# All router logits of a Mamba, MLP and mixture-of-experts layer on VectorE instead of TensorE

## The chip, the core and the metric

The kernel runs on one core of one Trainium2 chip. The metric is the device time of one execution in microseconds (us). All data is fp32. The engines are called as the profile calls them: PE (TensorE, the matrix multiplies), PEld (its weight loads), DVE (VectorE), ACT (ScalarE), POOL (GpSimd) and SP (SyncE, which here only issues DMAs). Each engine runs its own instructions in order and waits for the others through semaphores.

## What is computed

The input is one sequence of 2048 tokens with 512 channels. Two layers follow each other, each behind a layer norm and with a residual:

```python
x = L0_attn_hidden_states
x = x + _L0_attn_ref(_layernorm(x, axis=-1), ...)   # Mamba2 mixer, then a gated MLP
x = x + _L0_ffn_ref(_layernorm(x, axis=-1), Wr, Wg, Wu, Wd)
```

The first layer is a Mamba2 mixer (projection to 2576 columns, causal convolution of four taps, chunked state-space scan with 16 heads and chunks of 128 tokens, gated norm, output projection) and an MLP with 2048 hidden channels. The second is a mixture of eight experts with 352 hidden channels, of which every token takes two:

```python
router_logits = jnp.einsum('bsh,he->bse', x, Wr)       # x: normed tokens, Wr: 512 x 8
probs = jax.nn.softmax(router_logits.astype(jnp.float32), axis=-1)
topk_w, topk_idx = jax.lax.top_k(probs, K)             # K = 2
topk_w = topk_w / jnp.sum(topk_w, axis=-1, keepdims=True)
...
h = jax.nn.silu(g) * u                                  # g, u: x through Wg, Wu of each expert
y = jnp.einsum('besi,eih->besh', h, Wd)
out = jnp.einsum('bse,besh->bsh', combine.astype(x.dtype), y)
```

The change is about the first line only: the 2048 x 8 router logits.

## The kernel before, in words

**Stages.** Tokens are handled in tiles of 128 (on the partitions). The mixer runs in 8 blocks of 256 tokens (`mamba`, two `chunk`s each), the MLP in 4 blocks of 512 tokens (`feed_forward(fb)`, `fb` = 0 to 3, four tiles each). The MLP of block `fb` is interleaved with the mixer of the following tokens; the last MLP block stands after the mixer, next to the loads of the expert weights (`load_expert`). Then come the expert tiles (`tiles`, 36 slots of 128 gathered tokens), which add their output to `out` by indirect DMA.

**Order.** Both stages are Python generators that yield after a piece of work. `advance` moves the MLP on by one step per step of the mixer. PE keeps the program's order from the third mixer block on (`tc.manual_schedule`); the other engines and SP's DMA queue are ordered by a scheduler that estimates when each instruction can run. `tc.high_priority(AT_ONCE)` and `tc.issue_after(x)` bend that order by hand.

**The MLP block.** It has 16 parts `c` of 128 hidden channels, four steps each. A part is seven products of a 2 x 2 block scheme (`product`, L735), into two PSUM banks `x1` and `x2`. VectorE adds or multiplies the results: L768 (`p3`), L794 (`up`), L762 (`p2`) and L799. POOL multiplies gate by up (L800). From the third part on, two parts at a time are multiplied by the down weights (`mlp_down`, L719), and VectorE adds that to the token rows (L720). The weights come in through SP: `mg` (early, L534) and `ms` (late, L547) share three buffers, `md` (L552) has four. The mixer's weights `wi` (L99) have three. In the first block `mg` and `ms` are built from `w_gu`.

**The router, the end of each MLP block.** `route(fb, rows)` runs as the `tail` beside the next MLP block, one step of it per four steps of that block. It takes the layer norm of each tile (`normed`, L603), writes the normed tile `xn` to DRAM (`xnd`, and `xnd1` for blocks 0 to 2) and the residual to `out`. For blocks 0 to 2 it transposes `xn` on PE (four transposes, L201), copies the result to `xT` on ACT (L203), and multiplies it by the router's weights `wr_sb` (L612, four matmuls with 8 columns, recorded as 8), whose result DVE copies out (L613). For block 3 it computes logits on DVE: for each expert `e`, row `wr_rows[e]` is spread over all partitions (`cols`, L630), and `dot` (L616) multiplies a tile by it and sums. Then `top` picks two experts, matmuls with `tri` and `ones` (`pr`, L682 and L683) count the tokens ahead of each token, and POOL scatters token lists to DRAM (L697).

**From lists to experts.** `table(NS1, "1")` continues the tail of block 2: it makes the tile table of the first 16 expert slots, loads the lists (L1003) and ends with `idx` (L1014), by which POOL gathers the tokens of the first slots (L1054). This has to be ready when block 3's MLP ends.

**Buffers.** `mid` is a pool of three 2 KB (per partition) buffers, for `xn`, `xT`, small tables and the experts' `eh`. `row` has five. `params` holds convolution weights, biases, norms and the `D` vector in 116 columns and is loaded at the start.

Of the kernel before, what the change touches and what calls it, by code (L numbers as in the profile page):

```python
# [9 lines left out]
F32 = mybir.dt.float32  # L10
I32 = mybir.dt.int32
AF = mybir.ActivationFunctionType
ALU = mybir.AluOpType
# [33 lines left out]
EPS = 1e-5  # L47


C_CW, C_CB, C_NW, C_D, C_L1, C_L2, C_DTB, C_AL = 0, 48, 60, 68, 76, 80, 84, 100  # L50
NPAR = 116


@with_exitstack
def mamba_mlp_moe(ctx, tc, x, w_in, w_out, w_gu, w_down, par, wr, wr_rows, wg, wu, wd, out):

# [26 lines left out]
        nc.sync.dma_start(out=res[t], in_=x[t * P : (t + 1) * P, :])  # L83

    params = pw.tile([P, NPAR], F32, name="params")
    w_dt = pw.tile([P, NK, NH], F32, name="w_dt")
    w_o = pw.tile([P, 8, D], F32, name="w_o")
    wr_sb = const.tile([P, NK, NE], F32, name="wr_sb")

    for t in range(2 * NCH):  # L90
        load_x(t)
# [8 lines left out]
        return w  # L100

    ahead = [load_w_in(pair) for pair in range(2)]
    nc.sync.dma_start(out=wr_sb, in_=wr.rearrange("(k p) e -> p k e", p=P))


    ident = const.tile([P, P], F32, name="ident")
# [288 lines left out]
    def chunk(b, j, dt, ncum, dtdec, cd, cum, ec, xb, cs, zs):  # L395
# [9 lines left out]
        for gp in range(2):  # L405

            if t:
                with tc.issue_after(summed), tc.high_priority(AT_ONCE):
                    nc.gpsimd.tensor_tensor(ec[:, gp], ec[:, gp], cs[gp][:, :, tok], ALU.mult)
# [39 lines left out]
            if gp == 0 and t < NT - 1:  # L449
                pst = ps_tr.tile([P, 2, 4, HD], F32, name=f"pst{t}", tag="tr")  # L450
                for g in range(4):
                    nc.tensor.matmul(pst[halves[g % 2], g // 2], xbt[:, 1, g, :], xd[:, g], start=True, stop=True)


            yd = wa.tile([P, 4, P], F32, name=f"yd{t}_{gp}", tag="y")
            for i in range(4):
                at = C_D + 4 * gp + i
                nc.vector.scalar_tensor_tensor(
                    yd[:, i, :], xb[:, gp, tok], params[:, at : at + 1], py[:, i, :], ALU.mult, ALU.add
                )  # L460
            nc.vector.tensor_tensor(y[:, 4 * gp : 4 * gp + 4, :], yd, y[:, 4 * gp : 4 * gp + 4, :], ALU.mult)

# [50 lines left out]
        transposed(h, h2T[fb][:, half, :, off : off + P], params[:, C_L2 : C_L2 + NK])  # L513

# [55 lines left out]
    nc.gpsimd.memset(zero, 0.0)  # L570
# [15 lines left out]

    def route(fb, rows):

        mv2, rs2 = small("mv2", NJ, 2), small("rs2", NJ)
        for j in range(NJ):  # L590
            stats(small_p, rows[j], mv2[:, j, :])
# [3 lines left out]
        if fb == NFB - 1:  # L595

            kept = wk.tile([P, NJ, D], F32, name="kept", tag="h2T", bufs=1)

        def normed(j):
            t = fb * NJ + j  # L600
            nc.scalar.dma_start(out=out[t * P : (t + 1) * P, :], in_=rows[j])
            xn = kept[:, j] if fb == NFB - 1 else mid([D], f"xn{t}")
            nc.vector.tensor_scalar(xn, rows[j], mv2[:, j, 0:1], rs2[:, j : j + 1], ALU.subtract, ALU.mult)  # L603
            nc.scalar.dma_start(out=xnd[t * P : (t + 1) * P, :], in_=xn)
            if fb < NFB - 1:
                nc.scalar.dma_start(out=xnd1[t * P : (t + 1) * P, :], in_=xn)
            return xn

        def logits(j, xT):
            pl = bank("d", [NE], f"pl{fb}_{j}")  # L610
            for k in range(NK):
                nc.tensor.matmul(pl, xT[:, k, :], wr_sb[:, k, :], start=(k == 0), stop=(k == NK - 1))  # L612
            nc.vector.tensor_copy(lg[:, j, :], pl)  # L613

        def dot(product, xn, col, j, e):
            nc.vector.scalar_tensor_tensor(  # L616
                product, xn, 1.0, col, ALU.mult, ALU.mult, accum_out=lg[:, j, e : e + 1]
            )

        if fb == NFB - 1:  # L620

# [5 lines left out]
            for e in range(NE):  # L627
# [1 line left out]
                    cols = pmlp.tile([P, 2, D], F32, name=f"cols{e}", tag="mg", bufs=3)  # L629
                    nc.sync.dma_start(out=cols, in_=bc(wr_rows[e : e + 2], 0, P))  # L630
                for j in range(NJ):

                    with tc.issue_after(turning):
                        dot(pmlp.tile([P, D], F32, name="dot", tag="md", bufs=4), kept[:, j], cols[:, e % 2], j, e)
# [79 lines left out]

    def mlp_down(fb, rows, j, pair):

        pd = bank("d", [D], f"pd{fb}_{j}")
        for m, (a, d) in enumerate(pair):
            nc.tensor.matmul(pd, a[:, j * P : (j + 1) * P], d, start=(m == 0), stop=(m == 1))  # L719
        nc.vector.tensor_tensor(rows[j], rows[j], pd, ALU.add)  # L720

    def feed_forward(fb):

        nonlocal mlp_w, newest
        if fb == 0:
            w = load_early(0, 0)
            mlp_w = w, load_late(0, 0, w)
# [15 lines left out]
        for c in range(NFC):  # L743
# [13 lines left out]
            x2 = bank("u", [FH], f"py{fb}_{c}")  # L757

            def p2():
                product(x2, late[:, 2], b21)  # L760
                with tc.high_priority(AT_ONCE):
                    nc.vector.tensor_tensor(a[:, 0], a[:, 0], x2, ALU.add)  # L762
                nc.scalar.activation(a[:, 0], a[:, 0], AF.Silu)

            def p3():
                product(x2, late[:, 1], b22, False)
                with tc.high_priority(AT_ONCE):
                    nc.vector.tensor_tensor(a[:, 1], a[:, 1], x2, ALU.add)  # L768
                nc.scalar.activation(a[:, 1], a[:, 1], AF.Silu)

            def p5():
# [19 lines left out]
            yield  # L791
            product(x1, late[:, 0], t3, False)
            with tc.high_priority(AT_ONCE):
                nc.vector.tensor_tensor(up, up, x1, ALU.add)  # L794
            order[2]()
            yield
            product(x1, late[:, 3], t4, False)
            with tc.high_priority(AT_ONCE):
                nc.vector.tensor_tensor(a[:, 0], a[:, 0], x1, ALU.mult)  # L799
# [37 lines left out]
    def weigh(n):  # L837

        for m in unweighted[:n]:
            tc.keep_in_program_order(  # L840
                nc.gpsimd.tensor_scalar_mul(w_o[:, m, :], w_o[:, m, :], params[:, C_NW + m : C_NW + m + 1])
            )
        del unweighted[:n]

# [60 lines left out]
    def advance():  # L905
# [158 lines left out]
    def hidden(s, xT):  # L1064
# [6 lines left out]
        for k in range(NK):  # L1071
# [153 lines left out]
```

## Time and profile before

| what | value |
|---|---|
| time, median of 3 runs | 1542.44 us (1539.53 to 1543.87) |
| profiled execution, time | 1538.42 us |
| its span | 1536.6 us |
| PE busy | 1494.7 us, 97% of the span |
| DVE busy | 766.3 us, 50% |
| ACT busy | 741.8 us, 48% |
| POOL busy | 425.3 us, 28% |
| DMA | 219.63 MB, mean 143 GB/s |
| mean granted clock of TensorE | 0.993 |

The profile is of one execution. The span is the time from the first to the last instruction; 1.8 us of the time lie around it. A line of a group names the kernel's line, the engine, the operation and the tiles (`out<-in`); after `x` stands how often. In the row of 40 slices each digit is the busy share of 38.4 us in tenths. A matmul in fp32 is recorded as two passes, except the transposes. Numbers in brackets behind an instruction are idle time of its engine ahead of it, with what ended it. `PEclk` or the column behind the engines is the granted clock as a share of full speed.

### The profile page before, as it was taken

To read this page: it belongs to the slowest core of one execution; us is meant where nothing else is said; L and a number is where in the kernel's file an instruction comes from. 1 tells how busy PE (TensorE), PEld (TensorE's weight loads), DVE (VectorE), ACT (ScalarE), POOL (GpSimd) and SP (SyncE) were. 2 spreads that over 40 slices of the span, in tenths; PEclk is the share of its full clock that TensorE was granted. 3 is DMA by queue.
4 is the path that set the end of the run, shared out by engine and by line. 5 is a ranking of instruction groups with operands and counts; after the bars stand their busy time and mean duration, and the time that the engine had idled before them with its cause. 6 is when DMAs were issued, how large, how long until landed. Compare 5 with 4: busy or idle time off the path is not lost. (4 is left out here: it accounts for less than half of the span.)

```text
span 1536.6 us, 18795 instructions
## 1 busy us (share of the span) xinstructions
PE 1494.7 (97%) x6105; PEld 1016.5 (66%) x6105; DVE 766.3 (50%) x1999; ACT 741.8 (48%) x1328; POOL 425.3 (28%) x537
## 2 busy tenths in 40 slices
PE   8899999999999999999999999999999999999996
PEld 6656567677667676767676677666776666656553
DVE  7676875645545564556545544435343345322221
ACT  5887976735663598457755754222221121211110
POOL 3442324423342212141213120411121123433321
PEclk9999999999999999999999999999999999999999
DMA  9443445545454553454435442426879643443332
GB/s 297 127 157 117 145 134 182 196 144 168 164 170 148 179 167 128 131 126 137 145 96 193 150 138 81 103 77 200 296 228 242 209 119 64 61 73 67 64 62 35
DMA packets 128817, 219.63 MB, mean 143 GB/s; under 512 B 12624, under 2 KB 72912, under 8 KB 128720
## 3 DMA queue, kind: packets, MB, share of 16 engines
q1 hardware_dynamic: 105952, 168.44, 36.0%
q0 software_dynamic: 9088, 18.91, 7.3%
q10 hardware_dynamic: 13680, 31.07, 5.4%
q8 instruction: 51, 0.84, 0.2%
q14 instruction: 46, 0.38, 0.1%
HBM read 177.58 MB, written 40.80 MB: 142 GB/s over the span
## 5 line engine op out<-in xcount | busy, mean ns | idle before, releaser
L719 PE MATMUL pd<-md,a 128*128 128x512 f32 x512 | 239.8, 595 | 0.8 <-DVE r L720 0.7
L340 PE MATMUL pm<-hT,wi 128*128 128x256 f32 x768 | 187.0, 389 | 3.8 <-DMA wi<-in_w_in 3.8
L720 DVE TENSOR_TENSOR r<-r,pd 128x512 f32<-128x512 f32 x128 | 87.5, 684 | 151.7 <-PE pd L719 150.9
L340 PEld LDWEIGHTS pm<-hT,wi 128*128 128x128 f32 x768 | 143.0, 193 | 29.7 <-issue 11.1
L719 PEld LDWEIGHTS pd<-md,a 128*128 128x128 f32 x512 | 97.4, 191 | 77.4 <-issue 66.6
L361 DVE SCALAR_TENSOR_TENSOR ca<-pre,params,ca 128x256 f32<-128x256 f32 x288 | 139.5, 541 | 0.3
L735 PE MATMUL py<-h2T,ms 128*128 128x256 f32 x512 | 131.7, 379 | 2.4 <-DMA ms<-late 1.7
L800 POOL TENSOR_TENSOR a<-a,up 128x256 f32<-128x256 f32 x64 | 47.1, 736 | 267.3 <-DVE up L794 234.4
L340 PE MATMUL pz<-hT,wi 128*128 128x256 f32 x512 | 117.0, 381 | 0.0
L490 PE MATMUL po<-w_o,zs 128*128 128x512 f32 x256 | 114.5, 600 | 0.0
L1074 PE MATMUL epg<-ew,xgT 128*128 x288 | 109.0, 460 | 0.2 <-issue 0.2
L1074 PE MATMUL epu<-ew,xgT 128*128 x288 | 108.7, 459 | 0.0
L735 PEld LDWEIGHTS py<-h2T,ms 128*128 128x128 f32 x512 | 95.5, 190 | 18.1 <-issue 2.4
L420 ACT ACT_TABLE_LOAD x75 | 96.2, 1283 | 21.0 <-DVE ncum L285 14.1
L340 PEld LDWEIGHTS pz<-hT,wi 128*128 128x128 f32 x512 | 94.8, 190 | 13.8 <-issue 0.8
L1096 PE MATMUL epd<-ew,ehT 128*128 (+1 forms) x216 | 99.0, 594 | 1.0 <-DVE ehT L1089 1.0
L420 ACT ACTIVATE cum<-cum,ncum 128x128 f32<-128x128 f32 x256 | 85.7, 392 | 6.0 <-POOL cum L314 4.4
L490 PEld LDWEIGHTS po<-w_o,zs 128*128 128x128 f32 x256 | 48.9, 192 | 57.4 <-issue 56.1
L780 ACT COPY a<-px 128x256 f32<-128x256 f32 x64 | 23.6, 369 | 129.3 <-PE px L735 112.4
L1054 POOL DMA_INDIRECT xg<-xnd,idx x36 | 35.6, 988 | 161.3 <-PE pt L201 157.0
L422 DVE SCALAR_TENSOR_TENSOR cum<-cum,dt,psc 128x128 f32<-128x128 f32 x256 | 72.9, 339 | 5.3 <-PE psc L414 3.0
L1074 PEld LDWEIGHTS epu<-ew,xgT 128*128 128x128 f32 x288 | 54.7, 190 | 30.5
(243 smaller groups left out, 2503.3 us busy)
## 6 DMA issues: line engine op xcount, KB each, us to landing
wi<-in_w_in SPq DMA_DIRECT2D x80, 512.0 KB
ms<-late SPq DMA_DIRECT2D x48, 512.0 KB
mg<-early SPq DMA_DIRECT2D x48, 384.0 KB
md<-in_w_down SPq DMA_DIRECT2D x64, 256.0 KB
cum<-rowsd SPq DMA_DIRECT2D x32, 512.0 KB
late<-ms ACTq DMA_DIRECT2D x16, 512.0 KB
ec<-rowsd SPq DMA_DIRECT2D x60, 128.0 KB
mg<-in_w_gu SPq DMA_DIRECT2D x48, 128.0 KB
```

The costliest lines, as they stand in the source:

```text
L340: nc.tensor.matmul(pm[:, m, :], w[:, k, m * P : (m + 1) * P], hT[:, k, :], start=(k == 0), stop=(k == NK - 1))
L361: nc.vector.scalar_tensor_tensor(ca, pre[:, m, k : k + TB], cw[:, k : k + 1], ca, ALU.mult, ALU.add)
L420: nc.scalar.activation(lt[:, half, i], lt[:, half, i], AF.Exp, bias=ncum[:, j, h : h + 1])
L422: nc.vector.scalar_tensor_tensor(lt[:, half, i], lt[:, half, i], dt[:, j, h : h + 1], psc[:, half, i], ALU.mult, ALU.mult)
L490: nc.tensor.matmul(po, y[:, m, :], w_o[:, m, :], start=(m == 0), stop=(m == 7))
L719: nc.tensor.matmul(pd, a[:, j * P : (j + 1) * P], d, start=(m == 0), stop=(m == 1))
L720: nc.vector.tensor_tensor(rows[j], rows[j], pd, ALU.add)
L735: nc.tensor.matmul(ps, w[:, k], m[:, k], start=(first and k == 0), stop=(k == KH - 1), skip_group_check=True)
L800: nc.gpsimd.tensor_tensor(a[:, 1], a[:, 1], up, ALU.mult)
L1054: nc.gpsimd.indirect_dma_start(out=xg, out_offset=None, in_=src, in_offset=bass.IndirectOffsetOnAxis(ap=idx[:, n : n + 1], axis=0))
L1074: nc.tensor.matmul(ps, xT[:, k, :], w[:, lo : lo + EI], start=(k == 0), stop=(k == NK - 1))
L1096: nc.tensor.matmul(pd, hT[:n, m, :], w[:n, NG + m * D : NG + (m + 1) * D], start=(m == 0), stop=(m == len(ET) - 1))
```

## The change

- The router's logits of blocks 0, 1 and 2 are computed by VectorE, as those of block 3 are. The transposes, the copies to `xT`, the router's matmuls and the copies of `pl` go, and with them the tile `wr_sb`.
- Blocks 0 and 1 go a tile at a time: the fourth tile first, whose `xn` is still in SBUF, then the other three, each read back from DRAM (`again`). For each of the 32 pairs of tile and expert the router's row is loaded again (`column`), and the product is written over it.
- Block 2 takes two tiles at a time (2 and 3, then 0 and 1 read back), with 8 columns for each pair of tiles and the product in a buffer of its own.
- A column's buffer is one of two (`col`); `mid` shrinks from three buffers to one, and the experts' `eh` moves to `col`.
- While there are dots to do (`quick`), the tail takes a step at every step of the MLP block and not at every fourth.
- Each dot is ordered after `turning`, now the latest VectorE instruction of the MLP block.
- `params` is split: `norm_w`, `D` and `ln2_w` go to `params2`, which is loaded in the place of `wr_sb`.

```diff
-    wr_sb = const.tile([P, NK, NE], F32, name="wr_sb")
+    params2 = pw.tile([P, NPAR2], F32, name="params2")
...
-    nc.sync.dma_start(out=wr_sb, in_=wr.rearrange("(k p) e -> p k e", p=P))
+    nc.sync.dma_start(out=params2, in_=par2)
...
     def mid(shape, name):
-        return wk.tile([P, *shape], F32, name=name, tag="mid", bufs=3)
+        return wk.tile([P, *shape], F32, name=name, tag="mid", bufs=1)
+
+    def col(name, shape=(D,)):
+        return wk.tile([P, *shape], F32, name=name, tag="col", bufs=2)
...
+        def place_of(j):
+            if fb == NFB - 1:
+                return kept[:, j]
+            if j == NJ - 1:
+                return row(f"xn{fb}_{j}") if fb == NFB - 2 else mid([D], f"xn{fb}_{j}")
+            if j == NJ - 2 and fb == NFB - 2:
+                return mid([D], f"xn{fb}_{j}")
+            return col(f"xn{fb}_{j}")
...
-        def logits(j, xT):
-            pl = bank("d", [NE], f"pl{fb}_{j}")
-            for k in range(NK):
-                nc.tensor.matmul(pl, xT[:, k, :], wr_sb[:, k, :], start=(k == 0), stop=(k == NK - 1))
-            nc.vector.tensor_copy(lg[:, j, :], pl)
+        def dot(product, xn, weights, j, e):
+            with tc.issue_after(turning):
+                nc.vector.scalar_tensor_tensor(
+                    product, xn, 1.0, weights, ALU.mult, ALU.mult, accum_out=lg[:, j, e : e + 1]
+                )
+
+        def column(e):
+            w = col(f"col{e}")
+            nc.sync.dma_start(out=w, in_=bc(wr_rows[e], 0, P))
+            return w
+
+        def again(j, into):
+            t = fb * NJ + j
+            nc.sync.dma_start(out=into, in_=xnd[t * P : (t + 1) * P, :])
+            return into
...
+        elif fb == NFB - 2:
+            for j in range(2):
+                normed(j)
+            yield
+            pair = [normed(2), normed(3)]
+            yield
+            quick = True
+            for j in (2, 0):
+                if j == 0:
+                    pair = [again(0, mid([D], "xa")), again(1, row("xb"))]
+                    yield
+                    yield
+                product = row("dot")
+                w = column(0)
+                for e in range(NE):
+                    w, now = column(e + 1) if e < NE - 1 else None, w
+                    for n in range(2):
+                        dot(product, pair[n], now, j + n, e)
+                    if j or e < NE - 1:
+                        yield
+            quick = False
         else:
-            xn = normed(0)
-            yield
             for j in range(NJ):
-                if j:
-                    logits(j - 1, xT)
-                xT = mid([NK, P], f"xT{fb}_{j}")
-                transposed(xn, xT)
-                if j < NJ - 1:
-                    xn = normed(j + 1)
-                yield
-            logits(NJ - 1, xT)
+                xn = normed(j)
+                if j % 2:
+                    yield
+            quick = True
+            turns = [(j, e) for j in (NJ - 1, *range(NJ - 1)) for e in range(NE)]
+            w = column(0)
+            for n, (j, e) in enumerate(turns):
+                now, w = w, column(turns[n + 1][1]) if n < len(turns) - 1 else None
+                if e == 0 and n:
+                    xn = again(j, mid([D], f"xa{j}"))
+                    yield
+                    yield
+                dot(now, xn, now, j, e)
+                if n < len(turns) - 1:
+                    yield
+            quick = False
...
-                    nc.vector.tensor_tensor(a[:, 1], a[:, 1], x2, ALU.add)
+                    turning = nc.vector.tensor_tensor(a[:, 1], a[:, 1], x2, ALU.add).ins
...
-        if now[1] % 4 == 1:
+        if quick or now[1] % 4 == 1:
             next(tail, None)
...
-        if n % 4 == 2:
+        if quick or n % 4 == 2:
             next(tail, None)
...
-        h = mid([EI], f"eh{s}")
+        h = col(f"eh{s}", [EI])
```

The same assignment to `turning` is made at the other four VectorE instructions of the MLP block (L720, L762, L794, L799 of the kernel before).

More of the change, by code (lines that the diff above doesn't have):

```diff
@@ L47, with mamba_mlp_moe @@
 EPS = 1e-5
-C_CW, C_CB, C_NW, C_D, C_L1, C_L2, C_DTB, C_AL = 0, 48, 60, 68, 76, 80, 84, 100
-NPAR = 116
+C_CW, C_CB, C_L1, C_DTB, C_AL = 0, 48, 60, 64, 80
+NPAR = 96
+C_NW, C_D, C_L2 = 0, 8, 16
+NPAR2 = 20
 @with_exitstack
-def mamba_mlp_moe(ctx, tc, x, w_in, w_out, w_gu, w_down, par, wr, wr_rows, wg, wu, wd, out):
+def mamba_mlp_moe(ctx, tc, x, w_in, w_out, w_gu, w_down, par, par2, wr_rows, wg, wu, wd, out):
     nc = tc.nc
@@ L458, in chunk @@
                 nc.vector.scalar_tensor_tensor(
-                    yd[:, i, :], xb[:, gp, tok], params[:, at : at + 1], py[:, i, :], ALU.mult, ALU.add
+                    yd[:, i, :], xb[:, gp, tok], params2[:, at : at + 1], py[:, i, :], ALU.mult, ALU.add
                 )
@@ L512, in chunk @@
         half, off = divmod(off, FH)
-        transposed(h, h2T[fb][:, half, :, off : off + P], params[:, C_L2 : C_L2 + NK])
+        transposed(h, h2T[fb][:, half, :, off : off + P], params2[:, C_L2 : C_L2 + NK])
     KH = NK // 2
@@ L587, in route @@
     def route(fb, rows):
+        nonlocal quick
         mv2, rs2 = small("mv2", NJ, 2), small("rs2", NJ)
@@ L601, in normed @@
             nc.scalar.dma_start(out=out[t * P : (t + 1) * P, :], in_=rows[j])
-            xn = kept[:, j] if fb == NFB - 1 else mid([D], f"xn{t}")
+            xn = place_of(j)
             nc.vector.tensor_scalar(xn, rows[j], mv2[:, j, 0:1], rs2[:, j : j + 1], ALU.subtract, ALU.mult)
@@ L607, in normed @@
             return xn
-        def logits(j, xT):
-            pl = bank("d", [NE], f"pl{fb}_{j}")
-            for k in range(NK):
-                nc.tensor.matmul(pl, xT[:, k, :], wr_sb[:, k, :], start=(k == 0), stop=(k == NK - 1))
-            nc.vector.tensor_copy(lg[:, j, :], pl)
[L615 to L618, printed above, removed]
+        def dot(product, xn, weights, j, e):
[11 more added lines that the diff above has]
+            return into
         if fb == NFB - 1:
@@ L631, in route @@
                 for j in range(NJ):
-                    with tc.issue_after(turning):
-                        dot(pmlp.tile([P, D], F32, name="dot", tag="md", bufs=4), kept[:, j], cols[:, e % 2], j, e)
+                    dot(pmlp.tile([P, D], F32, name="dot", tag="md", bufs=4), kept[:, j], cols[:, e % 2], j, e)
                     if j == 1 or j == 3 and e < NE - 1:
                         yield
-        else:
-            xn = normed(0)
-            yield
+        elif fb == NFB - 2:
[19 more added lines that the diff above has]
+            quick = False
+        else:
             for j in range(NJ):
-                if j:
-                    logits(j - 1, xT)
-                xT = mid([NK, P], f"xT{fb}_{j}")
-                transposed(xn, xT)
-                if j < NJ - 1:
-                    xn = normed(j + 1)
-                yield
-            logits(NJ - 1, xT)
+                xn = normed(j)
[13 more added lines that the diff above has]
+                    yield
+            quick = False
         chosen = [small(n, NJ, NE) for n in ("o1", "o2")]
@@ L715, in mlp_down @@
     def mlp_down(fb, rows, j, pair):
+        nonlocal turning
         pd = bank("d", [D], f"pd{fb}_{j}")
@@ L719, in mlp_down @@
             nc.tensor.matmul(pd, a[:, j * P : (j + 1) * P], d, start=(m == 0), stop=(m == 1))
-        nc.vector.tensor_tensor(rows[j], rows[j], pd, ALU.add)
+        turning = nc.vector.tensor_tensor(rows[j], rows[j], pd, ALU.add).ins
     def feed_forward(fb):
-        nonlocal mlp_w, newest
+        nonlocal mlp_w, newest, turning
         if fb == 0:
@@ L759, in p2 @@
             def p2():
+                nonlocal turning
                 product(x2, late[:, 2], b21)
                 with tc.high_priority(AT_ONCE):
-                    nc.vector.tensor_tensor(a[:, 0], a[:, 0], x2, ALU.add)
+                    turning = nc.vector.tensor_tensor(a[:, 0], a[:, 0], x2, ALU.add).ins
                 nc.scalar.activation(a[:, 0], a[:, 0], AF.Silu)
             def p3():
+                nonlocal turning
                 product(x2, late[:, 1], b22, False)
                 with tc.high_priority(AT_ONCE):
-                    nc.vector.tensor_tensor(a[:, 1], a[:, 1], x2, ALU.add)
+                    turning = nc.vector.tensor_tensor(a[:, 1], a[:, 1], x2, ALU.add).ins
                 nc.scalar.activation(a[:, 1], a[:, 1], AF.Silu)
@@ L793, in feed_forward @@
             with tc.high_priority(AT_ONCE):
-                nc.vector.tensor_tensor(up, up, x1, ALU.add)
+                turning = nc.vector.tensor_tensor(up, up, x1, ALU.add).ins
             order[2]()
@@ L798, in feed_forward @@
             with tc.high_priority(AT_ONCE):
-                nc.vector.tensor_tensor(a[:, 0], a[:, 0], x1, ALU.mult)
+                turning = nc.vector.tensor_tensor(a[:, 0], a[:, 0], x1, ALU.mult).ins
             nc.gpsimd.tensor_tensor(a[:, 1], a[:, 1], up, ALU.mult)
@@ L840, in weigh @@
             tc.keep_in_program_order(
-                nc.gpsimd.tensor_scalar_mul(w_o[:, m, :], w_o[:, m, :], params[:, C_NW + m : C_NW + m + 1])
+                nc.gpsimd.tensor_scalar_mul(w_o[:, m, :], w_o[:, m, :], params2[:, C_NW + m : C_NW + m + 1])
             )
@@ L1189 @@
             columns(cb),
-            columns(paired(a["norm_w"], 0)),
-            columns(paired(np.repeat(a["D"], HD), 0)),
             columns(a["ln1_w"]),
-            columns(a["ln2_w"]),
             np.broadcast_to(a["dt_bias"], (P, NH)),
@@ L1197 @@
         axis=1,
+    )
+    par2 = np.concatenate(
+        [columns(paired(a["norm_w"], 0)), columns(paired(np.repeat(a["D"], HD), 0)), columns(a["ln2_w"])], axis=1
     )
@@ L1207 @@
         "par": par,
-        "wr": a["Wr"],
+        "par2": par2,
         "wr_rows": a["Wr"].T,
```

## The prediction

> **What bounds the kernel now.** I read the page first (share of each engine, busy by slice), then the TensorE groups with shapes kept apart, the order in time around one router step, the busy time by stage, and single lines for prices.
>
> ```profile
> span 1536.6 us, 18795 instructions
> PE 1494.7 (97%) x6105; PEld 1016.5 (66%) x6105; DVE 766.3 (50%) x1999; ACT 741.8 (48%) x1328; POOL 425.3 (28%) x537
> PE   8899999999999999999999999999999999999996
> DVE  7676875645545564556545544435343345322221
> DMA  9443445545454553454435442426879643443332
> ```
>
> TensorE is the bound almost from end to end. VectorE is half busy and thins out towards the end; DMA is low except in slices 28 to 32, where the expert weights are fetched.
>
> ```profile
> 560.00:740.00 180.00, 179.45 (x782) 126.89 (x781) 101.19 (x285) 126.24 (x207) 41.35 (x55) 1.00 0.47 142
> 860.00:1020.00 160.00, 160.00 (x678) 111.36 (x677) 75.71 (x215) 68.09 (x133) 34.98 (x42) 1.00 0.40 117
> 1080.00:1140.00 60.00, 60.00 (x260) 44.65 (x259) 22.95 (x64) 16.72 (x37) 6.30 (x19) 1.00 0.81 271
> ```
>
> These are the busy times (PE, its weight load, DVE, ACT, POOL, clock, DMA share, GB/s) of the three stretches in which blocks 0, 1 and 2 are routed. PE is full in all three and its granted clock is 1.00, so a microsecond of PE work taken out is a microsecond of span, if no new wait arises. The third is different in one thing: DMA is at 0.81.
>
> **What goes from TensorE.** The order in time shows the true pitch of the router's instructions (busy time overstates it, since matmuls overlap):
>
> ```profile
> 560.42 1.88 PE L719 MATMUL pd<-md,a 128*128 128x512 f32 x4
> 562.13 0.95 PE L612 MATMUL pl<-wr_sb,xT 128*128 128x8 f32 x8
> 562.94 0.63 PE L201 MATMUL pt<-ident,xn 128*128 128x128 f32 x4
> 563.41 1.03 PE L735 MATMUL px<-h2T,mg 128*128 128x256 f32 x4
> ```
>
> From start to start, the four logits matmuls of a tile (recorded as 8 passes) take 562.94 - 562.13 = 0.81 us, its four transposes 563.41 - 562.94 = 0.47 us. Blocks 0 to 2 have twelve tiles: 12 x (0.81 + 0.47) = 15.3 us. In the built order PE loses exactly these 96 instructions; the rest keep their order, but for the two `pr` matmuls of each block and those of the first table, which come later. The Trainium skill ("TensorE: Matmul & The Clock Gate", section "Back-to-back issue gap") puts a sustained pair of weight load and matmul at about 81 ns for 128 columns. With that, 96 passes and 48 transposes would be 144 x 0.081 = 11.7 us. The rows above say 101 ns a pass and 117 ns a transpose; I take 15.3.
>
> **What is added on VectorE.** 12 tiles x 8 experts = 96 dots. The last block already does such dots:
>
> ```profile
> L616 DVE SCALAR_TENSOR_TENSOR dot<-kept,cols x32: 684/686/690, 1242.8 to 1301.2; 128x512 f32<-128x512 f32 x32
> L616 DVE DVE_READ_ACCUMULATOR dot<-kept,cols x32: 80/82/84, 1243.4 to 1301.8; 128x1 f32 x32
> ```
>
> 96 x 0.69 = 66 us, against twelve small copies (L613, 0.16 us each) removed. Blocks 0 and 1 get 32 dots each: 22 us in stretches of 180 and 160 us, where DVE goes from 0.56 to about 0.68 and from 0.47 to 0.61. There is room on average; the price is the order. DVE runs in order, and where a matmul needs its next result at once, a dot in front delays PE by up to 0.69 us. The dots are tied behind the latest result that PE is about to need (`turning`), so I let one in eight hit, with half its length or a little more: 64/8 x 0.4 = 3 us. The ends: 0, and one in two at 0.35: 11 us.
>
> Block 2 is tighter. Its eight steps per half run through the last MLP block, where VectorE's own work per four steps is this:
>
> ```profile
> 1150.23 0.42 DVE L768 TENSOR_TENSOR a<-a,py 128x256 f32<-128x256 f32 x1 [1.11 <-issue]
> 1151.09 0.42 DVE L794 TENSOR_TENSOR up<-up,px 128x256 f32<-128x256 f32 x1 [0.44 <-PE px L735]
> 1151.88 0.42 DVE L762 TENSOR_TENSOR a<-a,py 128x256 f32<-128x256 f32 x1 [0.37 <-issue]
> 1153.19 0.42 DVE L799 TENSOR_TENSOR a<-a,px 128x256 f32<-128x256 f32 x1 [0.89 <-PE px L735]
> 1154.57 0.69 DVE L720 TENSOR_TENSOR r<-r,pd 128x512 f32<-128x512 f32 x1 [0.96 <-PE pd L719]
> 1157.91 0.69 DVE L720 TENSOR_TENSOR r<-r,pd 128x512 f32<-128x512 f32 x1 [2.65 <-PE pd L719]
> 1159.86 0.42 DVE L768 TENSOR_TENSOR a<-a,py 128x256 f32<-128x256 f32 x1 [1.26 <-PE py L735]
> ```
>
> A group takes about 9.6 us here (1150.23 to 1159.86), 2.4 us a step; 3.1 us of it is busy. Two dots a step add 8 x 0.69 = 5.5 us: 8.6 of 9.6. It fits only if no dot waits for its column.
>
> **The columns.** Each dot (each pair in block 2) needs one router row spread over 128 partitions: 64 + 16 columns, and 8 tiles read back, 88 DMAs of 256 KB on SP's queue: 22 MB on 219.63. SP issues one in about 0.4 us (L552's and L534's rows: 0.32 to 0.46), 35 us in all, and it mostly waits for PE now. From the trace's packet records I counted bytes behind each issue: a 256 KB load lands 2.3 to 4.9 us after issue in the first two stretches, and 2.9 to 5.6 us in the third (5.5 when it stands behind two expert loads of 704 KB).
> - Blocks 0 and 1: two buffers, one dot per step of some 5 us: 10 us from a release to the next use of the buffer, against 0.4 + 4.9. No wait. A column on SP waits for an earlier dot, and weight loads queue behind it; from landing to the first matmul, `ms` has 7 to 21 us to spare there, `mg` 9 to 30, `wi` 19 to 48. Cost 0; if SP were held by over 7 us, `ms` would be late next.
> - Block 2: a column's buffer is released by the second dot of a pair (1.4 us), the next load lands L later, and the pair after next must start two steps (4.8 us) on. So L up to 4.8 - 1.5 = 3.3 us is free; beyond that every second pair falls back by L - 3.3. A half has eight pairs, four turns of which the first is loaded ahead. At L = 4 a half ends 3 x 0.7 = 2.1 us late, at 5.5 it ends 6.6 late. DVE blocks in order, and L768, L794, L762 and L799 stand behind. Between the matmuls that L768 or L794 takes up and the next that write the same bank lie four others, 0.86 us, and the instruction uses nearly all of that: 0.1 us to spare. L762 and L799 have over 1. The 18 loads also bring 18 x 128 packets of 98 ns (this queue's 2 KB packets there) / 16 = 14 us of DMA time into 43 us that are 0.8 full, so they fill it. `ms` has a median of 6.5 us to spare and once 1.2. I take L near 4.5, where a half ends 3.6 us late; some 1 us of that falls into gaps like the 2.65 ahead of L720, so it costs 2.5, 5 us for both. Ends: 1 and 18.
>
> **The shared read port** speaks against the change. A GpSimd product has 1258 ns as minimum and 1912 as maximum:
>
> ```profile
> L409 POOL TENSOR_TENSOR ec<-ec,cs x30: 1258/1272/1912, 76.1 to 974.3; 128x512 f32<-128x512 f32 x30
> ```
>
> The excess, 0.65 us, is about the length of one VectorE instruction. The Trainium skill ("SBUF — State Buffer", section "Who interferes with whom") says that a VectorE instruction with two SBUF inputs and a GpSimd instruction that reads SBUF exclude each other for the whole instruction; each dot has two. POOL is busy for 23% of the first stretch, so some 96 x 0.25 = 24 dots would meet one, at 0.35 us: 8 us if all of it reached PE. But the median of L409 is 14 ns over its minimum beside a DVE that is half busy, and POOL mostly waits (L800: 234 us for L794). I take 0 to 1 inside the 3 us above, and 8 as the end.
>
> **The rest, one price each.** ACT loses twelve copies (0.59 us each) and, in the built order, 11 of 248 table loads (1.28 each): hidden, it is half idle. `params2` (10 KB) takes `wr_sb`'s place (16 KB in 32-byte pieces) at 4.7 us on SP: PE's first wait for a weight is at 35.7 us, for a load issued at 27.6 or later, so 0, within 0.5. The third tile's `xn` of blocks 0 and 1 waits until the first tile's two stores have landed; they were issued 0.6 and 1 us after it (L604, L606) and nothing needs DVE for 2.7 us then: 0, at worst 1 each. The list scatters on POOL are moved, not added. The first table comes four steps (9.5 us) later: its gathers, issued at 1213.46 and 1214.80 with their last packets at 1218.3, would end at about 1227.8, before the transposes at 1230.47. This cover is down to 2.7 us; without it PE would wait for the excess. The `eh` tiles get two buffers for three; a tile's `eh` is transposed during the next tile, so 0.
>
> **Sum.** -15.3 + 3 + 5 + 0 = -7.3 us. The profiled execution took 1538.4 us (span 1536.6, 1.8 around it), 4 below the median of 1542.4; so it would be 1531 there, and 1535 against the median.
>
> **Rivals.**
> 1. Nearly all of it arrives: columns land in time and dots fit the gaps: -15.3 + 2, 1529. For: a full PE and a DVE at half load. Against: block 2's DMA share.
> 2. It cancels: one dot in three delays PE by 0.35 (11 us for 96) and late columns cost 3: -1.3, 1541. For: many DVE results are taken by PE at once (L768, L794, L799).
> 3. Slower, by one mechanism: in block 2 a column takes 6 us from release to landing, because it stands behind expert loads in a queue that the columns themselves fill. A pair then slips 2.7 us in each turn, three turns 8 us, both halves 16; the stall also keeps SP on columns while `ms`, with 6.5 us to spare, waits behind them: 4 more. -15.3 + 3 + 20 = +8, 1550. It decides from about 5.6 us on, when block 2 costs over 17. For: 5.5 us was seen before any column was there. Against: expert loads have 24 us or more to spare and fall back by themselves when SP is held.
> That PE's work stays is excluded by the built order.
>
> **Numbers.** About 0.3% (4.6 us) is what a measurement of this kernel tells from no change. Chances: the central case 0.36 (own range 1531 to 1538), rival 1 0.21, rival 2 0.22, rival 3 0.21. Faster: 0.57, same: 0.22, slower: 0.21. The likeliest is 1535; the range 1527 to 1549 takes in rival 1 and most of rival 3.
>
> **What would show it.** Right: PE without the rows of L612 and of `xn`; DVE at about 0.65 in the first two stretches, few waits of dots for columns there; in block 2, DVE waits for `col` of 0.5 to 1 us each and PE waits for L822, L848 or L853 (the new numbers of L768, L794, L799), 5 us in all. Wrong: dots that wait for columns in blocks 0 and 1, PE waits for `wi` or `ms`, or transposes of `xg` that wait for the first gather.

## The result and the profile after

The changed kernel takes **1555.33 us** (median of 5 runs, 1548.95 to 1562.61), the kernel before 1543.87 us beside it (1539.53 to 1545.56). The ratio is **1.0078** with a 95% interval of 1.0053 to 1.0103: slower by some 12 us. The prediction said 1535 and faster. The profiled execution took 1548.95 us against 1538.42 before, 10.5 more; it lies at the low end of its runs, and every sum below is made against it.

The page of the changed kernel, the lines that answer to those of before:

```profile
span 1547.2 us, 18836 instructions
PE 1485.1 (96%) x5961; PEld 1002.6 (65%) x5961; DVE 830.0 (54%) x2179; ACT 720.7 (47%) x1305; POOL 432.3 (28%) x537
PE   7999999999999999999998999998989999999996
DVE  7676875645645576558655654554563355322221
DMA  9443445545544745566356554449888643443332
```

TensorE lost its 144 instructions (6105 to 5961) and is busy for less time, yet the span is longer: it waits. The PE row shows where: before it was a nine from slice 2 to slice 38 (counted from 0), now there are eights in slices 21, 27 and 29. The last two (1044 to 1083 and 1122 to 1160 us) lie in the stretch where block 2 is routed beside the last MLP block. VectorE rises from 3 and 4 tenths to 5 and 6 in slices 28 and 29.

The busy times by stage (PE, PEld, DVE, ACT, POOL, clock, DMA share, GB/s), the same three stretches as before:

```profile
560.00:740.00 180.00, 179.90 (x763) 127.29 (x762) 120.67 (x331) 119.52 (x199) 38.50 (x50) 1.00 0.58 182
860.00:1020.00 160.00, 159.28 (x640) 107.26 (x639) 96.11 (x263) 60.82 (x124) 30.29 (x35) 1.00 0.52 164
1080.00:1140.00 60.00, 52.46 (x190) 36.65 (x191) 33.08 (x88) 10.65 (x28) 7.33 (x16) 0.97 0.88 294
```

Blocks 0 and 1 look as forecast: PE stays full with DVE at 0.67 and 0.60. In block 2 PE is busy for 52.5 of 60 us, where it was full, and its clock is 0.97.

To see the loss in microseconds I took, in both traces, the distance from the start of each matmul to the start of the next, the median of its kind as its price, and what lies above as stall. The sum of prices fell from 1514.2 to 1497.8 us (-16.4). The stall rose from 75.6 to 101.3 us (+25.7). (Price and stall add up to more than the span, because distances below the median are not taken off: 67 us before, 66 after. With that difference, -16.4 and +25.7 come within 0.1 us of the 10.5 of the profiled executions.)

| stretch | stall before | stall after | difference |
|---|---|---|---|
| 0 to 461 us | 43.8 | 44.4 | +0.6 |
| 461 to 960 us (block 0 and part of block 1 routed) | 21.1 | 24.1 | +3.0 |
| 960 to 1037 us | 1.5 | 2.6 | +1.1 |
| 1037 to 1229 us (block 2 routed) | 5.7 | 26.6 | **+21.0** |
| behind 1229 us | 3.4 | 3.3 | 0 |

What the waits in block 2 are, is seen from the tile `col` in the window of its dots (it has the DMA's time from issue to landing), and from the waits of the same window (us in total, times, longest):

```profile
L635 SPq DMA_DIRECT2D col<-in_wr_rows x16: 327/328/477, 1081.7 to 1141.2; - x16
DMA to landing us min/median/max: 3.4/5.4/7.5
...
DVE dot L629 <- DMA col<-in_wr_rows: 13.8, 9, 3.8
...
PE py L787 <- DVE a L822: 9.6, 5, 3.0
```

A column lands 5.4 us after its issue in the median. Nine pairs of dots wait 13.8 us for one, and PE waits five times, 9.6 us, for L822, the sum that stands behind the dots on VectorE. The longest of PE's five waits, in order of time (lines left out at the dots):

```profile
1112.68 0.69 DVE L629 SCALAR_TENSOR_TENSOR dot<-xn,col 128x512 f32<-128x512 f32 x1 [0.87 <-DMA col<-in_wr_rows]
...
1113.41 0.33 SPq L641 DMA_DIRECT2D xa<-xnd  x1
...
1114.79 0.38 SPq L537 DMA_DIRECT2D mg<-early  x1
...
1115.22 0.90 SPq L635 DMA_DIRECT2D col<-in_wr_rows  x2
...
1116.21 0.38 SPq L1008 DMA_DIRECT2D ew<-in_wd  x1
...
1122.46 0.69 DVE L629 SCALAR_TENSOR_TENSOR dot<-xa,col 128x512 f32<-128x512 f32 x1 [3.04 <-DMA col<-in_wr_rows]
...
1123.20 0.69 DVE L629 SCALAR_TENSOR_TENSOR dot<-xb,col 128x512 f32<-128x512 f32 x1
...
1123.82 0.41 DVE L822 TENSOR_TENSOR a<-a,py 128x256 f32<-128x256 f32 x1
...
1124.28 2.08 PE L787 MATMUL py<-h2T,ms 128*128 128x256 f32 x4 [3.00 <-DVE a L822]
```

The column is issued at 1115.22 and the dot starts at 1122.46, over 7 us later. VectorE has nothing to do for 3 us, and L822 (its `py` was complete before) stands behind the two dots. PE then waits 3.00 us for L822. This is the change from the first half of block 2 to the second. The two dots on the last column that used this buffer had ended by 1111.1, but SP's queue stood from 1108.7 to 1113.41 at `xa`: its one `mid` buffer held tile 2, which the dot of 1112.68 still read. The column went out behind `xa`, `md`, `xb` and `mg` and landed at 1122.38, 7.2 us after its issue.

### The profile page after: what moved, and what is told of

The parts are those of the page before. It is cut to its first block, busy times and chain, and to the rows that moved or that the text cites. A ratio compares the mean times of both kernels' runs of the same rounds, so it can differ in the third digit from the quotient of the medians.

```text
span 1547.2 us, 18836 instructions
## 1 busy us (share of the span) xinstructions
PE 1485.1 (96%) x5961; PEld 1002.6 (65%) x5961; DVE 830.0 (54%) x2179; ACT 720.7 (47%) x1305; POOL 432.3 (28%) x537
## 2 busy tenths in 40 slices
DMA packets 141106, 242.69 MB, mean 157 GB/s; under 512 B 13648, under 2 KB 73936, under 8 KB 141008
## 5 line engine op out<-in xcount | busy, mean ns | idle before, releaser
L1128 PE MATMUL epg<-ew,xgT 128*128 x288 | 109.0, 460 | 0.3 <-ACT xgT L206 0.3
L1128 PE MATMUL epu<-ew,xgT 128*128 x288 | 108.7, 459 | 0.0
L343 PEld LDWEIGHTS pz<-hT,wi 128*128 128x128 f32 x512 | 94.8, 190 | 13.8 <-issue 0.8
L834 ACT COPY a<-px 128x256 f32<-128x256 f32 x64 | 23.6, 369 | 128.2 <-PE px L787 116.7
L317 POOL TENSOR_SCALAR_AFFINE_SELECT cum<-cum 128x1024 f32<-128x1024 f32 x32 | 36.4, 1139 | 157.0 <-DMA cum<-rowsd 109.0
L787 PE MATMUL px<-h2T,mg 128*128 128x256 f32 x256 | 68.3, 390 | 7.7 <-DVE a L853 6.1
```

The costliest lines, as they stand in the source:

```text
L317: nc.gpsimd.affine_select(out=c, in_=c, pattern=[[0, 8], [1, P]], compare_op=ALU.is_ge, fill=-3.0e38, base=0, channel_multiplier=-1,)
L343: nc.tensor.matmul(pm[:, m, :], w[:, k, m * P : (m + 1) * P], hT[:, k, :], start=(k == 0), stop=(k == NK - 1))
L787: nc.tensor.matmul(ps, w[:, k], m[:, k], start=(first and k == 0), stop=(k == KH - 1), skip_group_check=True)
```

## The experiments

All ratios are to the kernel before, run beside each, with their 95% intervals. Two theories at first: (1) the loss sits in block 2 and comes from late columns; (2) the dots as such are in VectorE's way, in all blocks.

**Blocks 0 and 1 alone** (`b01_vector`; block 2 takes the code of before, with `xn` in `col` and `xT` in `mid`; the new branch stands ahead of the change's own for block 2, which is then never reached, and `wr_sb` is loaded again):

```diff
+            if fb == NFB - 2:
+                return col(f"xn{fb}_{j}")
...
+        elif fb == NFB - 2:
+            xn = normed(0)
+            yield
...
+            logits(NJ - 1, xT)
         elif fb == NFB - 2:
```

> Blocks 0 and 1 as in the changed kernel, block 2's logits on TensorE as before. Theory 1 (the loss sits in block 2: columns land 5 to 6 us after their buffer is released, VectorE waits in order, TensorE waits for L822): eight tiles of TensorE work go, 8 x 1.37 = 10.9 us; given back some 3 us by dots in front of other results and 3.6 us by block 1's list scatters, which still fall on a load of ms near 1040 us. So 4 to 8 us faster than before, ratio 0.995 to 0.9975. Theory 2 (the dots as such cost: VectorE is in the way everywhere, 25.7 us of new TensorE stall over 96 dots): 64 dots cost 17 us, so +6 us, ratio 1.004.

Measured: 1533.65 us, ratio **0.9966 (0.9954 to 0.9978)**: faster. The sum of prices falls by 11.1 us, the stall between 461 and 960 us rises by 2.9. The profiled run has one new stall of 4.4 us at 1064, discussed with the list scatters below.

**Block 2 alone** (`b2_vector`; the same with the condition `fb < NFB - 2`).

> Block 2 as in the changed kernel, blocks 0 and 1 on TensorE as before. Theory 1: -5.5 us of TensorE work, +12 us of waits for L822 (with the clock dip behind the longest), +2 for stores on ACT, +2 for block 2's later list scatters: about 11 us slower than before, ratio 1.006 to 1.009. Theory 2: 32 of 96 dots, 8.6 - 5.5 = +3 us, ratio 1.002.

Measured: 1552.72 us, ratio **1.0096 (1.0077 to 1.0115)**: some 15 us slower, at least as much as the whole change. Its tile `col` and its waits:

```profile
DMA to landing us min/median/max: 4.8/5.8/7.8
...
DVE dot L639 <- DMA col<-in_wr_rows: 18.0, 10, 4.7
PE py L809 <- DVE a L844: 12.2, 5, 4.7
```

(L844 is L822 in this kernel.) Columns land still later, and the waits grow with them. Stall between 1037 and 1229 us is 25.9 against 5.7 before; 20.2 less 5.3 of prices is 14.9, about the measured loss. The two halves of the change, -0.34% and +0.96%, add up to +0.62%, within the interval of the whole. Theory 2 is refuted: it asked for 17 us of stall from the dots of blocks 0 and 1, and the whole stall there rose by 2.9.

**A third column buffer in block 2** (`cols3`): the dots' product goes to a PSUM bank, its SBUF buffer in the pool of `row` becomes a column (and later that of every second `xg`), and a column is asked for two pairs ahead.

```diff
-            w = col(f"col{e}")
+            if fb == NFB - 2 and e % 3 == 2:
+                w = more_rows.tile([P, D], F32, name=f"col{e}", tag="col3", bufs=1)
+            else:
+                w = col(f"col{e}")
...
-                product = row("dot")
-                w = column(0)
+                product = bank("tr", [D], f"dot{j}")
+                ws = [column(0), column(1)]
```

> The changed kernel with three column buffers for block 2 in place of two (the dots' product goes to a PSUM bank, its buffer becomes the third column): a column is asked for two pairs ahead. Theory 1: dots that wait for a column fall from 13.8 us to under 4, TensorE's waits for L822 from 9.6 us to under 3; 10 us faster than the changed kernel, ratio to the kernel before 0.999 to 1.002. Theory 2 (two dots a step are too much for VectorE there): waits for L822 stay over 6 us although columns are there, ratio over 1.005.

Measured: 1541.72 us, ratio **1.0022 (1.0010 to 1.0034)**, 0.56% better than the change and just above the forecast of theory 1. The waits between 1075 and 1160 us:

```profile
PE pd L776 <- DMA md<-in_w_down: 3.2, 1, 3.2
...
PE py L792 <- DVE a L827: 1.1, 1, 1.1
DVE dot L629 <- DMA col<-in_wr_rows: 1.1, 1, 1.1
```

The dots' waits fall from 13.8 to 1.1 us, PE's waits for this sum (here L827) from 9.6 to 1.1, with just as many dots. So it was the late column, not VectorE's load. (The wait that is left stands at the change from the first half to the second.) A new wait stands ahead of the others: `md`, 3.2 us. SP's queue shows why:

```profile
1116.17 2.21 SPq L638 DMA_DIRECT2D col<-in_wr_rows  x2
1118.43 0.43 SPq L1011 DMA_DIRECT2D ew<-in_wg  x1
1118.91 0.50 SPq L555 DMA_DIRECT2D md<-in_w_down  x1
```

Two columns take 2.21 us, where their issues take 0.33 each: SP stands at a column whose buffer is not free, and the `md` that PE waits for from 1122.8 to 1126.0 is issued behind it.

**Columns of block 2 on ScalarE's queue** (`cols3_act`):

```diff
-            nc.sync.dma_start(out=w, in_=bc(wr_rows[e], 0, P))
+            queue = nc.scalar if fb == NFB - 2 else nc.sync
+            queue.dma_start(out=w, in_=bc(wr_rows[e], 0, P))
```

> The kernel with three columns in block 2, the columns of block 2 issued by ScalarE's queue in place of SP's. If what was left there came from SP held at columns that wait for their buffer (md issued at 1118.9 and waited for 3.2 us, ms 3.9 us), these waits fall to the 1.7 us of the kernel before, and the time by 4 us: ratio to the kernel before 0.999 to 1.000. If it came from the bytes alone, the waits for md and ms stay over 5 us, ratio 1.002. ScalarE held at a column would show as TensorE waits for L834 or L841.

Measured: 1537.43 us, ratio **0.9995 (0.9982 to 1.0007)**, 0.27% or 4 us better than `cols3`: the wait for `md` is gone; the waits for `ms` between 1037 and 1229 us fell from 3.9 to 2.9, not to the 1.7 expected. ScalarE was held once at a dot (2.9 us); in the same window TensorE waited 0.6 us for L847 (L841 in this kernel) and not for L840 (L834).

**Expert loads held back** (`late_experts`):

```diff
-        if n % 5 in (0, 2) and parts:
+        if n > 24 and n % 3 < 2 and parts:
```

> The changed kernel with the 24 expert loads held back until step 25 of the last feed-forward block and then issued two in three steps, so that none is in flight beside block 2's columns. If the expert loads are what makes a column late (theory 1a), columns land in about 4 us rather than 5.4, dots wait under 5 us for them in all and TensorE under 4 us for L822. If the columns are slow of themselves (1b), both stay as they are (13.8 and 9.6 us). The whole time tells less: after step 25 the expert loads come denser and can be late themselves; from 10 us faster than the changed kernel to 10 us slower.

Measured: 1549.45 us, ratio 1.0072 (1.0052 to 1.0092). The tile `col` and the waits between 1075 and 1160 us:

```profile
DMA to landing us min/median/max: 4.3/4.4/4.7
...
DVE dot L629 <- DMA col<-in_wr_rows: 9.5, 9, 1.8
...
PE py L787 <- DVE a L822: 4.0, 3, 2.2
```

This is between 1a and 1b: without expert loads beside it a column takes 4.4 us with hardly any spread, so 1.0 of 5.4 us and the long ones go with the expert loads. But 4.4 is still more than two buffers hide, and 9.5 us of waits remain, in portions small enough (1.8 at most) that less than half of them reaches PE. The total says nothing here: at 1175 us PE waited 6.6 us for an `md` behind the denser expert loads.

**The list scatters, moved.** In the change, the eight list scatters of block 1 run at 1037.6 to 1047.4 us, at the end of the block; before they ran at 964 to 979. Two yields ahead of `pr` cost eight steps, since `quick` is off again. In the changed kernel a wait of 1.99 us for `ms` follows at 1052 (none before), in `b01_vector` ScalarE waited 13.7 us for its stores `out<-r` and PE 4.2 for ScalarE. Theory 3: this is a cost of its own. The test lets `quick` stand to the end of the router of blocks 0 and 1, so that two steps pass, not eight (`b01_early` on `b01_vector`, `after_early` on the change; the last line is the end of `route`):

```diff
                 if n < len(turns) - 1:
                     yield
-            quick = False
...
             yield
+        quick = False
```

> Blocks 0 and 1 on VectorE, block 2 on TensorE, and the list scatters of blocks 0 and 1 two fast steps behind the last dot in place of two slow ones (8 steps). Theory 3 (the later list scatters are a cost of their own: in the kernel before they ran at 964 to 979 us, in the changed kernel and in the one with blocks 0 and 1 alone at 1033 to 1047, just before block 1 ends, and their small packets held up a load of ms in the one and the stores of r, and with them ScalarE, in the other): the stall of 4.36 us at 1064 and its slow clock fall to the 0.4 us of the kernel before, 4 to 6 us less: 1528 to 1530, ratio to the kernel before 0.993 to 0.994. Rival (the stores were late for another reason, the scatters don't matter): no change, ratio 0.9966.

> The changed kernel with the same earlier list scatters of blocks 0 and 1 and nothing else. Theory 3: no wait for ms near 1052 us (2.15 us and 1.5 us of slow clock in the changed kernel), some 3.6 us less, ratio to the kernel before 1.005; block 2's waits for L822 stay at 9 to 12 us. Rival: as the changed kernel, 1.008.

Measured: 0.9976 (0.9965 to 0.9987) and 1.0098 (1.0068 to 1.0128). Neither is better than without it. The stalls at 1052 and 1064 are gone in both, and the stall of 1037 to 1075 us is the 2.9 of before; but PE now waits for `both` ahead of `pr` in blocks 0 and 1, 2.9 us in the one and 3.1 in the other, and runs at a slow clock behind the longer wait. VectorE needs 4.2 us from the end of the last dot (1011.98) to `both` (1016.18), and TensorE was at `pr` after 2.7 us. Block 2's wait for L822 stayed (9.3 us). `cols3_act_early`, the same on `cols3_act`:

> The same with the earlier list scatters of blocks 0 and 1. If all three causes are right (late columns, SP held, later scatters), all twelve tiles on VectorE give -16.4 us of TensorE work, +3 for dots, +2 for stores and small waits, +3 for the rest in block 2: ratio 0.994 to 0.997. If block 2 keeps a cost of over 5 us it stays behind the kernel with blocks 0 and 1 alone.

Measured: 1.0012 (1.0000 to 1.0025), outside the forecast as well.

Four steps (`b01_mid`, `cols3_act_mid`) and three (`b01_three`, `cols3_act_three`, with 3 in place of the 4):

```diff
-        yield
-        yield
+        for _ in range(4 if quick else 2):
+            yield
```

> Blocks 0 and 1 on VectorE, block 2 on TensorE, the list scatters of blocks 0 and 1 four fast steps behind the last dot (two were too few: TensorE waited 1.77 us for `both` ahead of pr and ran 1.7 us slower behind it; eight brought the scatters to the block's end). Theory 3 (later scatters cost 4 us, and the two fast steps only put another wait in their place): neither the wait for `both` nor the stalls at 1052 and 1064, 1529 to 1531, ratio to the kernel before 0.993 to 0.995. Rival (the scatters' place is no matter): 0.9966 as without it.

> All twelve tiles on VectorE, three columns in block 2, issued by ScalarE's queue, and the scatters of blocks 0 and 1 four fast steps behind the last dot. With all three causes of the loss gone: -16.4 us of TensorE work, +3 for dots of blocks 0 and 1, +4 left in block 2: ratio 0.993 to 0.996, beside or ahead of the kernel with blocks 0 and 1 alone. If the scatters' place is no matter: 0.9995 as without it.

Measured: 0.9988 (0.9975 to 1.0001) and 1.0010 (0.9999 to 1.0020): behind the 0.9966 and 0.9995 of the eight steps, and not apart from the two steps by more than the intervals. GpSimd's queue at the place (first column the start, second the duration in us):

```profile
1033.48 0.96 POOL L769 DMA_INDIRECT lists<-entries,to  x1 [0.30 <-issue]
1034.45 1.29 POOL L505 TENSOR_TENSOR x<-x,h 128x512 f32<-128x512 f32 x1
1035.91 0.98 POOL L769 DMA_INDIRECT lists<-entries,to  x1 [0.17 <-issue]
```

Four scatters are in front of L505, whose `h` was ready at 1031.1. The store behind L505 holds ScalarE, L838 (the activation of `a`) follows it, L875 waits for L838, and PE waits 4.8 us for L875.

> As the kernel with four fast steps, with three: `both` is ready one step (2.4 us) earlier than pr needs it, and all eight list scatters of a block stand ahead of L505's sum on GpSimd (with four, half of them stood behind it and half in front, L505 came late, the store behind it held ScalarE, and TensorE waited 4.8 us for L875). Theory 3: no wait for `both`, none for L875, none at 1052 and 1064: 1529 to 1531 where the kernel before has 1538.5, ratio 0.993 to 0.995. Rival (every place for the scatters costs about the same, only the engine that waits changes): 0.996 to 0.999.

> All twelve tiles on VectorE, three columns on ScalarE's queue in block 2, three fast steps. Theory 3: ratio 0.994 to 0.997; rival: 0.999 to 1.001, as with two steps, four and eight.

Measured: **0.9954 (0.9938 to 0.9970)**, 1534.34 us against 1541.30 for the kernel before, and 0.9983 (0.9971 to 0.9995). `b01_three` is the best kernel found, 7 us ahead of the kernel before. It falls just short of theory 3's 0.993 to 0.995, and PE waits 1.1 us for an `ms` at 1036 instead. Its interval overlaps that of `b01_vector`, so that the place of the scatters gains anything over the eight steps is not shown. Shown is that a bad place costs: the intervals of four steps (0.9988) and three (0.9954) lie apart; two steps (0.9976) overlap with both. With all twelve tiles on VectorE the best is 0.9983, between the two forecasts. Beside `b01_three` block 2 keeps a net cost of 4 to 5 us even with three columns; what it consists of is not settled.

## Why the prediction was wrong, point by point

- **TensorE's saving, -15.3.** Right in kind: 144 instructions went, and the sum of start-to-start prices fell by 16.4 us. That is 114 ns for each of the 144, near the trace's rows (101 and 117 ns); the 81 ns of the Trainium skill ("TensorE: Matmul & The Clock Gate", section "Back-to-back issue gap") had given an estimate of 11.7 us.
- **Dots in blocks 0 and 1, +3.** The number was right, partly by luck. The stall between 461 and 960 us rose by 3.0 in the change and by 2.9 in `b01_vector`, but in the change 2.4 of the 3.0 lie ahead of the first dot (566.98). In the stretches with dots (561 to 745 and 860 to 1020 us) it rose by 1.1 and 1.5. DVE is at 0.67 and 0.60 (forecast 0.68 and 0.61). Dots waited 6.4 us for columns in all, hardly any of which reached PE; the forecast was that they would not wait.
- **The third tile's `xn`, 0.** Wrong in block 0, where the wait for the stores was named:

```profile
529.78 0.55 DVE L620 TENSOR_SCALAR xn<-r,mv,rs 128x512 f32<-128x512 f32 x1 [3.21 <-DMA xnd<-xn]
```

  L853 stands behind it on VectorE, and PE waits 1.67 us for L853 (0.51 for the same sum before): 1.2 us of stall more.
- **The shared port, inside the 3.** It did show:

```profile
668.95 2.95 POOL L412 TENSOR_TENSOR ec<-ec,cs 128x512 f32<-128x512 f32 x2
668.99 1.78 DVE L629 SCALAR_TENSOR_TENSOR col<-xa,col 128x512 f32<-128x512 f32 x1
```

  Of the 64 dots in blocks 0 and 1, 13 took 739 to 1778 ns, 5.5 us over the median of 684 in sum, and each of them overlapped a TENSOR_TENSOR of GpSimd. None of the 43 dots without such an overlap took over 693. The medians hide it (684 ns for the dots, 1271 for GpSimd's L412 against 1272 before). Little of it reached PE: a wait of 0.72 us for L848 at 963.5 us stands behind a dot of 1602 ns.
- **Block 2's columns, +5. This is the term that failed.** The mechanism was the one written: columns land too late for two buffers, a pair falls back, and L822 stands behind. Its size was wrong: 12.2 us in place of 5 (10.4 of stall at L822, 1.8 of slow clock behind the longest wait). L was taken as 4.5 us; it was 5.4 in the median (5.8 with block 2 alone). The 4.5 came from loads seen before the columns had joined that queue. With 5.4 the prediction's own formula gives 3 x 2.1 = 6.3 us for a half, 12.6 for both. That the sum fits is partly luck: the first half lost 3.3 us, the second 7.1, and the largest single wait (3.2 of the 7.1) stands where the formula has none. It takes the first column of each half as loaded ahead; in the second half that column was held behind `xa` and landed after 7.2 us. And 1 us for a half was taken off for gaps in which the delay would be lost. PE had 0.1 us to spare at L822 by the prediction's own working.
- **Rival 3** named this course: from 5.6 us on, 16 + 4 for weights behind columns, 1550. The stall between 1037 and 1229 rose by 21.0, near its 20, but that is partly luck: 12.2 of it is at L822, and the rest stands mostly at the scatters, `mg`, `ms` and L841 (below), where the rival had weights behind columns. It got 0.21, although 5.5 us had been seen for a load behind two expert loads; and the range ended at 1549, below the rival's own 1550.
- **SP held by columns** was priced at 0 for blocks 0 and 1, rightly, and in block 2 within rival 3 alone. `cols3` against `cols3_act` shows 4 us for it with three buffers. With two it was not measured by itself.
- **"The list scatters are moved, not added", 0.** Wrong: the move itself had a price. In the change 2.15 us of stall at 1052 and 1.5 of slow clock stood behind block 1's scatters, and the stall at `mg` and `ms` after those of block 2 went from 1.9 to 4.0 us. That the scatters cause the first is supported by its absence in `after_early`; for the second it was not tried. No other place was shown to be cheaper on the whole.
- **ACT.** Table loads fell by eleven (248 to 237) at no gain, as said. Two waits of PE for L841 at 1072 and 1080 us, 2.0 us together, were not foreseen; they lie where `normed` now runs in two steps in place of four, and were not tried separately.
- **`params2`, the start, the first table.** Right at 0: stall up to 461 us is 44.4 against 43.8; PE waited 0.29 us at L1128 for the first tokens. The bytes were 23.06 MB more (219.63 to 242.69), not 22, which moves no term.

## What to carry to other kernels

Where a streamed operand feeds an engine that runs in order, price it by the landing time in that stage with the new loads in the queue, and set it against the free time of the ring of buffers: here 5.4 us against 3.3, and one column held behind another load, cost 12 us on an engine with 0.1 us to spare; with one more buffer, asked for two pairs ahead, 1.1 us of wait was left with no less work. Split a change by stage before judging it: two thirds of this one are a gain of 0.34%, the last third loses three times as much. A step that is moved in time takes its DMAs and its place in every queue with it; two, three and four steps of delay each made a wait at another place.

## What was not expected of the hardware

Behind some waits of 1.6 to 3 us TensorE's granted clock was halved. Busy times by 2 us, the eighth field is the granted clock:

```profile
1050.00:1052.00 2.00, 0.05 (x1) 0.08 (x1) 0.00 (x0) 0.37 (x1) 0.00 (x0) 1.00 0.93 33
1052.00:1054.00 2.00, 2.00 (x6) 1.60 (x7) 0.42 (x1) 0.06 (x1) 0.00 (x0) 0.65 0.90 109
1054.00:1056.00 2.00, 2.00 (x6) 1.60 (x5) 0.42 (x1) 0.35 (x1) 0.25 (x1) 0.50 0.87 72
1056.00:1058.00 2.00, 2.00 (x8) 1.39 (x8) 1.05 (x3) 0.42 (x1) 0.48 (x1) 1.00 0.85 41
```

After 1.99 us without work the matmuls came 0.43 us apart in place of 0.22 for some 3.5 us, and 1.5 us were lost on top of the wait. The same followed the wait of 3.00 us at 1124, in `b01_early` one of 1.77 us, and in both kernels one of 1.6 us near 209 us, but not those of 2.14 at 1149 and 2.76 at 1190. So the length of the wait alone does not decide.

The rows above also show the DMA engines 0.9 busy at 33 to 109 GB/s behind the list scatters, where columns and expert loads reach 294 GB/s at 0.88. The scatters' own packets (4 and 64 bytes) are not what fills them: all packets of up to 64 bytes between 1037 and 1058 us add up to 0.3 us of the 16 engines' time. It is the packets of `ms` (4096 bytes) that last longer, 0.87 us in the mean there; in the kernel before, without scatters in that stretch, packets of that size took 0.22, and 0.64 between 964 and 985, where its own scatters are.

A dot whose product goes to PSUM takes 695 ns against 691, and its accumulator read 142 ns against 81.
